# Output stage of a triangle update: the channel mean by narrow products and a subtraction, the residual added on GpSimd

## The chip, the cores and the metric

The kernel runs on one core of a Trainium2 chip. The metric is the device time of one execution in microseconds. Engines are named as in the profile: PE is TensorE, DVE is VectorE, ACT is ScalarE, POOL is GpSimd, and SP is the queue that issues most loads.

## What is computed

The input is an image of 256 x 256 positions with 128 channels in 32-bit floats. Four layers follow one another, each of the form x = x + layer(groupnorm(x)): an attention, a recurrence, a triangle update and a convolution. The change is in the triangle update's last part. Cut to what matters, the reference is:

```python
def _L2_conv_ref(pair, ...):
    pair_norm = layer_norm(pair, ln_in_w, ln_in_b)
    p = jnp.einsum('bijd,hd->bijh', pair_norm, p_in_w)
    g = jax.nn.sigmoid(jnp.einsum('bijd,hd->bijh', pair_norm, g_in_w))
    left = g[..., :H] * p[..., :H]
    right = g[..., H:] * p[..., H:]
    out = jnp.einsum('bikd,bjkd->bijd', left, right / jnp.float32(L))
    out = layer_norm(out, ln_out_w, ln_out_b)          # over the 128 channels
    out = jnp.einsum('bijh,dh->bijd', out, p_out_w)
    gate = jax.nn.sigmoid(jnp.einsum('bijd,ed->bije', pair_norm, g_out_w))
    return gate * out

# in reference():
x = x + _L2_conv_ref(_gn(x), ...)
x = x + _L3_conv_ref(_gn(x), ...)                       # the convolution, which needs x's statistics
```

The change concerns the last four lines of the layer and the residual addition: a layer norm over channels, the output product, the gate, the sum with x, and the statistics of this sum for the next group norm.

## The kernel before, in words

Channels lie on the 128 partitions, positions along the free dimension. The triangle update (method `triangle`) has three stages. The first normalises x (read from the DRAM image x2T) and writes the result to znT. The second makes left and right factors (`LR`) from znT and multiplies them; the result goes channel by channel, by stores that POOL issues, to the DRAM image prodD. The third, which the change rewrites, reads prodD, znT and x2T in 32 pieces of 2048 positions (`NB // 2`; a piece of one image is 1 MB) and writes the sum to x3T.

In the third stage all work on TensorE, VectorE and ScalarE is issued through helpers that keep the program's order (`mm`, `act`, `tt`, `stt`, `bn`, `table`), so each of these engines runs its instructions strictly as written. The loads on SP and the stores on POOL have no such tie: a scheduler places them, each in its queue's own order.

For piece p the loop does this:

- `load(p + 2)` fetches znT, prodD and x2T for two pieces ahead into tiles `zn`, `pr` and `xin`, three buffers each.
- `variance` multiplies the squares of the centred piece with `m32` (`tmean`, 128 x 32, every entry 1/128): four products of 512 columns, each into 32 partitions of one PSUM tile `var`, placed side by side in the array. Two ScalarE passes (logarithm, then exponential times -0.5) make 1/sigma, `rs`.
- `gates(p)`: product of `zn` with the gate weights (`pe`, L61 like all products), then a sigmoid on ScalarE into `ga`. It needs another table of functions than the logarithm, so each piece has two table loads.
- `spreads` brings `rs` back to all partitions: four products with 32 rows each (`tspread`), in two PSUM tiles `pr` of 1024 columns. (The name `pr` thus stands for a PSUM tile here and for the SBUF tile of the product above.)
- VectorE scales: `on` = `zs` times `pr`.
- `centre(p + 1)`: the product of the next piece with `cmat`, a full 128 x 128 matrix that subtracts the channel mean (`zc`); ScalarE copies it to `zs` and squares that into `sq`.
- `py`: the output product of `on`, then on VectorE `ga` = (`py` + bias) times `ga`, `x3` = `ga` + `xin`, and `bn` statistics of `x3`, 512 columns at a time.
- POOL issues the store of `x3` to x3T (L1361).

PSUM has two kinds of buffers here: tag `w`, three slots of 1024 columns, which `pe`, `pr`, `zc` and `py` take in turn, and tag `r`, two slots of 512 columns for `var`. A slot is taken again when its last reader is done. At piece 28, `early_statistics` combines the statistics so far on VectorE. After the last piece the convolution's group norm waits for all statistics. The tiles of this stage lie on the memory of the second stage's tiles: the first ones on the buffers of `zt` (loads of znT), the later ones on `LR`.

Of the kernel before, what the change touches and what calls it, by code (L numbers as in the profile page):

```python
# [9 lines left out]
F32 = mybir.dt.float32  # L10
AF = mybir.ActivationFunctionType
ALU = mybir.AluOpType
# [5 lines left out]
P = 128  # L18
# [8 lines left out]
LN_EXP = "natural_log_exp_and_others"  # L27
EXP_TANH = "exp_and_others"
SIGMOID = "sigmoid_and_others"


class Kernel:
# [21 lines left out]
    def act(self, out, in_, func, bias=0.0, scale=1.0, **kw):  # L54
        return self.nc.scalar.activation(out, in_, func, bias=bias, scale=scale, **kw)  # L55

    def table(self, name, key="table"):
        return self.chain(key, self.nc.scalar.preload_act_table_set(name))

    def mm(self, out, lhsT, rhs, start=True, stop=True):  # L60
        return self.nc.tensor.matmul(out, lhsT, rhs, start=start, stop=stop)  # L61
# [1067 lines left out]
    def triangle(self, x2T, x3T, znT, prodD, stats2, shift2, stats3, prepare):  # L1129
# [3 lines left out]
        nc, tc, I = self.nc, self.tc, self.i  # L1133
        V = nc.vector
        NB, G, CQ = NPIX // 1024, 4, P // 4
        pin = lambda f: lambda *a, **k: tc.keep_in_program_order(f(*a, **k))  # L1136
        mm, act, copy = pin(self.mm), pin(self.act), pin(nc.scalar.copy)
        tt, ts, stt, bn = pin(V.tensor_tensor), pin(V.tensor_scalar), pin(V.scalar_tensor_tensor), pin(V.bn_stats)
        table, add = pin(nc.scalar.preload_act_table_set), pin(V.tensor_scalar_add)
        flat = lambda t: t.rearrange("p k n -> p (k n)")  # L1140
        MUL, ADD = ALU.mult, ALU.add
        with ExitStack() as c:
            wp = c.enter_context(self.pool(name="tw", bufs=1))
            with self.pool(name="twp", bufs=2, space=PSUM) as ps0:
# [4 lines left out]
                wpg, oraw, we = W, W["o"], W["e"]  # L1149
                pb = ps0.tile([P, 2], F32, name="tpbo", tag="gn")  # L1150
                self.mm(pb[:, 0:1], oraw, lob)
                wbo = wp.tile([P, 1], F32, name="twbo")
                V.tensor_copy(wbo, pb[:, 0:1])
                wo = wp.tile([P, P], F32, name="two")
# [13 lines left out]
            m32 = wp.tile([P, 32], F32, name="tmean")  # L1168
# [4 lines left out]
            def variance(ps, work, sq):  # L1173

                var = ps.tile([P, 512], F32, name="var", tag="r", bufs=2)
                for k in range(4):
                    mm(var[32 * k:32 * k + 32], m32, sq[k // 2][:, (k % 2) * 512:(k % 2 + 1) * 512])
                rs = work.tile([P, 512], F32, name="rs")
                act(rs, var, AF.Ln, bias=self.eps)
                act(rs, rs, AF.Exp, scale=-0.5)  # L1180
                return rs

            def spreads(ps, rs):
                pr = [ps.tile([P, 1024], F32, name="pr", tag="w") for _ in range(2)]
                for k in range(4):
                    mm(pr[k // 2][:, (k % 2) * 512:(k % 2 + 1) * 512], spread[32 * k:32 * k + 32], rs[32 * k:32 * k + 32])
                return pr


            with ExitStack() as c1:  # L1190
                io = c1.enter_context(self.pool(name="t1", bufs=3))
                work = c1.enter_context(self.pool(name="t1w", bufs=4))
                ps = c1.enter_context(self.pool(name="t1s", bufs=3, space=PSUM))
                xin, sq, zs = {}, {}, {}

                def load(m):
                    if m < NB // 2:
                        xin[m] = io.tile([P, 2048], F32, name="xin")
                        nc.sync.dma_start(xin[m], x2T[:, m * 2048:(m + 1) * 2048])

                def centre(m, b):
                    if m >= NB // 2:
                        return
                    zc = ps.tile([P, 1024], F32, name="zc", tag="w")
                    for k in range(2):
                        s = b * 1024 + k * 512
                        mm(zc[:, k * 512:(k + 1) * 512], lc, xin[m][:, s:s + 512])
                    zs[m, b] = work.tile([P, 1024], F32, name="zs")
                    add(zs[m, b], zc, cb)
# [12 lines left out]
                for m in range(NB // 2):  # L1222
                    load(m + 2)
                    centre(m + 1, 0)
                    rs = variance(ps, work, [sq[m, b] for b in range(2)])
# [3 lines left out]
                    pr = spreads(ps, rs)  # L1229
# [44 lines left out]

            with ExitStack() as c1:
                io = c1.enter_context(self.pool(name="t3", bufs=3))
                work = c1.enter_context(self.pool(name="t3w", bufs=3))
                ps = c1.enter_context(self.pool(name="t3s", bufs=3, space=PSUM))
                D = [{} for _ in range(NB // 2)]

                def product(wt, src, h, name):
                    z = ps.tile([P, 2, 512], F32, name=name, tag="w")
                    for k in range(2):
                        mm(z[:, k], wt, src[:, h * 1024 + k * 512:h * 1024 + (k + 1) * 512])
                    return flat(z)

                def load(p):
                    if p < NB // 2:

                        for n, src in (("zn", znT), ("pr", prodD), ("xin", x2T)):  # L1290
                            t = D[p][n] = io.tile([P, 2048], F32, name=n)
                            for c0, c1 in ((0, 96), (96, P)) if n == "pr" and p == 0 else ((0, P),):
                                nc.sync.dma_start(t[c0:c1], src[c0:c1, p * 2048:(p + 1) * 2048])

                def centre(p):
                    if p < NB // 2:
                        d = D[p]
                        d["zs"], d["sq"] = [], []
                        for h in range(2):
                            zc = product(self.cmat, d["pr"], h, "zc")  # L1300
                            z = work.tile([P, 1024], F32, name="zs")
                            act(z, zc, AF.Copy)
                            d["zs"].append(z)
                            sq = work.tile([P, 1024], F32, name="sq")
                            act(sq, z, AF.Square)
                            d["sq"].append(sq)

                def stats(h):
                    for k in range(2):
                        o = h * 1024 + k * 512  # L1310
                        bn(stats3[:, 4 * p + 2 * h + k, :], x3[:, o:o + 512])

                def gates(p):
                    pe = [product(we, D[p]["zn"], h, "pe") for h in range(2)]
                    if p:
                        table(SIGMOID)
                    D[p]["ga"] = []
                    for h in range(2):
                        ga = work.tile([P, 1024], F32, name="ga")
                        act(ga, pe[h], AF.Sigmoid)  # L1320
                        D[p]["ga"].append(ga)

                load(0)
                load(1)
                gates(0)
                centre(0)
                table(LN_EXP)
                for p in range(NB // 2):
                    d = D[p]
                    load(p + 2)  # L1330
                    on, py, x3 = [], [], io.tile([P, 2048], F32, name="x3")
                    hs = [slice(h * 1024, (h + 1) * 1024) for h in range(2)]
                    rs = variance(ps, work, d["sq"])
                    if p:
                        gates(p)
                    pr = spreads(ps, rs)
                    for h in range(2):
                        on.append(work.tile([P, 1024], F32, name="on"))
                        tt(on[h], d["zs"][h], pr[h], MUL)
                    ga = d["ga"]  # L1340
                    centre(p + 1)
                    if p + 1 < NB // 2:
                        table(LN_EXP)
                    py = [product(wo, on[h], 0, "py") for h in range(2)]
                    last = p + 1 == NB // 2
                    if p == NB * 7 // 16:
                        self.early_statistics(stats3, "3")
                    gate = lambda h: stt(ga[h], py[h], wbo, ga[h], ADD, MUL)
                    if not last:
                        gate(0)  # L1350
                        gate(1)
                    for h in range(2):
                        if last:
                            gate(h)
                        tt(x3[:, hs[h]], ga[h], d["xin"][:, hs[h]], ADD)
                        if last:
                            stats(h)
                    for h in range(2):
                        if not last:
                            stats(h)  # L1360
                    nc.gpsimd.dma_start(x3T[:, p * 2048:(p + 1) * 2048], x3)  # L1361
                    d.clear()

    def transformed_taps(self, late, kt, wd, bv):

# [279 lines left out]
```

## Time and profile before

| What | us |
|---|---|
| median of 3 runs (4857.59 to 4860.5) | 4858.48 |
| profiled execution, whole | 4863.21 |
| its span, from the first to the last instruction | 4861.1 |
| PE busy in the span | 4680.3 (96%) |
| DVE busy | 3632.2 (75%) |
| ACT busy | 3331.2 (69%) |
| POOL busy | 1858.4 (38%) |

The profile page is one execution recorded by the hardware. A group of instructions is named by line, engine, operation and tiles (output, arrow, inputs); the line is that of the helper that issues it, so L61 stands for every product and L55 for most of ScalarE, and one goes by the tiles. The number after x is the count, and the mean duration follows in ns; then comes the idle time of the engine just before these instructions and who ended it. A product of 32-bit floats is issued as two passes, and weight loads and products are counted together in the chain, so four products of 512 columns appear as x8. The chain of waits goes back from the last instruction to whatever released it, and shows where time can be saved.

The third stage runs from 3899.5 to 4326.7 us of the span. In the timeline the first loads stand out: znT's first piece is issued at 3824.3, and the second part of prodD's first piece, which needs the last channel's store, at 3899.5.

### The profile page before, as it was taken

What the parts mean: (1) busy time and instruction counts of PE and PEld (TensorE: products, weight loads), DVE (VectorE), ACT (ScalarE), POOL (GpSimd) and SP (SyncE); (2) the same over time, 40 slices, a digit from 0 to 9 for tenths busy, and PEclk for the clock granted to TensorE, in tenths of its full rate; (3) what the DMA queues carried; (4) which work ended last, traced back from release to release, by engine and by line L of the source; (5) the groups of instructions that cost most, each with busy time, mean ns of one, the idle gap of its engine ahead of it and who ended that gap; (6) DMA issues with size and microseconds to landing.
All of it is one profiled execution on the core that took longest, in us unless ns stands there. A gap on an engine that the chain in (4) does not pass through costs nothing.

```text
span 4861.1 us, 78233 instructions
## 1 busy us (share of the span) xinstructions
PE 4680.3 (96%) x30415; PEld 2669.2 (55%) x30415; DVE 3632.2 (75%) x4551; ACT 3331.2 (69%) x5009; POOL 1858.4 (38%) x1294
## 2 busy tenths in 40 slices
PE   8999999999999899999999996999999999999999
PEld 2444555555555433333333332269999943369999
DVE  6676777777777699999999996763443367789886
ACT  6556888888888799999999995543333377752110
POOL 0344555555555376666666664421001100000000
PEclk9999999999999999999999998999999999999999
DMA  8893122222222245555555555986776598854432
GB/s 299 309 350 112 53 80 87 84 88 83 80 87 83 80 110 132 132 133 131 133 132 133 134 131 164 331 327 225 265 256 225 211 349 324 320 205 165 141 120 70
DMA packets 221153, 835.13 MB, mean 172 GB/s; under 512 B 59142, under 2 KB 62492, under 8 KB 172244
## 3 DMA queue, kind: packets, MB, share of 16 engines
q1 hardware_dynamic: 144606, 498.19, 29.9%
q0 software_dynamic: 74880, 331.50, 23.4%
q8 instruction: 244, 4.00, 0.3%
q14 instruction: 127, 1.04, 0.1%
q10 hardware_dynamic: 1296, 0.40, 0.0%
HBM read 497.84 MB, written 265.03 MB: 157 GB/s over the span
## 4 chain that ended last, share of the span: by engine, by line
PE 66%; ACT 14%; DVE 11%; issue 6%; DMA 2%; POOL 1%; SPq 0%; ACTq 0%; DVEq 0%; POOLq 0%
PE z L61 9%; PE m L61 8%; PE zc L61 7%; PE nd L61 7%; PE sc L61 6%; PE po L61 5%; PE ppq L61 3%; PE ppv L61 3%; PE pe L61 2%; PE ppg L61 2%; PE ppk L61 2%; PE px L61 2%; PE py L61 2%; PE var L61 2%; ACT L950 2%
## 5 line engine op out<-in xcount | busy, mean ns | idle before, releaser
L609 DVE TENSOR_TENSOR e<-sc,bT 128x1024 f32<-128x1024 f32 x512 | 613.2, 1218 | 255.9 <-PE sc L61 253.8
L609 POOL TENSOR_TENSOR ks<-e 128x1024 f32<-128x1024 f32 x256 | 601.4, 2367 | 443.0 <-PE nd L61 429.5
L55 ACT ACTIVATE e<-e 128x1024 f32<-128x1024 f32 x512 | 539.6, 1054 | 39.5 <-DVE e L609 29.9
L1136 DVE TENSOR_TENSOR LR<-z,sg 128x512 f32<-128x512 f32 x256 | 268.2, 1048 | 363.2 <-ACT sg L55 363.2
L61 PE MATMUL m<-U,v 128*128 128x128 f32 x4608 | 514.7, 275 | 0.0
L61 PEld LDWEIGHTS m<-U,v 128*128 128x128 f32 x4608 | 514.6, 192 | 0.0
L61 PE MATMUL z<-wf,zt 128*128 128x128 f32 x4096 | 458.4, 275 | 2.4 <-DVE zn L1136 1.4
L61 PEld LDWEIGHTS z<-wf,zt 128*128 128x128 f32 x4096 | 458.0, 192 | 3.6 <-DVE zn L1136 2.2
L55 ACT ACTIVATE sg<-z 128x512 f32<-128x512 f32 x256 | 152.8, 597 | 307.7 <-PE z L61 307.7
L1268 POOL DMA_DIRECT2D prodD<-o x128 | 69.0, 540 | 617.2 <-ACT o L55 607.4
L61 PE MATMUL sc<-proj 32*128 32x256 f32 x4096 | 300.1, 403 | 3.0 <-DVE e L609 2.2
L978 POOL TENSOR_TENSOR fs<-f 128x512 f32<-128x512 f32 x64 | 176.4, 2756 | 276.1 <-DVE f L975 256.5
L61 PEld LDWEIGHTS sc<-proj 32*128 32x128 f32 x4096 | 188.1, 185 | 160.9 <-PE px L61 94.8
L61 PE MATMUL nd<-e,proj 128*32 128x256 f32 x4096 | 272.3, 383 | 2.6 <-DVE og L609 2.6
L55 ACT ACTIVATE dn<-dn 128x512 f32<-128x512 f32 x384 | 237.8, 619 | 10.3 <-DVE dn L609 6.2
L978 POOL TENSOR_TENSOR u<-t,tr 128x512 f32<-128x512 f32 x64 | 232.4, 3632 | 11.1 <-DVE tr L981 9.7
L978 POOL TENSOR_TENSOR t<-t,v 128x1024 f32<-128x1024 f32 x64 | 209.6, 3275 | 51.9 <-DVE t L975 51.9
L61 PE MATMUL po<-LR 128*128 128x256 f32 x1024 | 222.1, 379 | 6.9 <-DVE LR L1136 6.9
L1521 ACT COPY m4s<-m 128x512 f32<-128x512 f32 x32 | 18.7, 585 | 290.5 <-PE m L61 290.5
L61 PEld LDWEIGHTS po<-LR 128*128 128x128 f32 x1024 | 194.2, 190 | 34.0 <-DVE LR L1136 7.7
L1531 POOL DMA_DIRECT2D out_dram<-ys x32 | 37.0, 1155 | 425.4 <-DVE ys L1529 425.4
L61 PE MATMUL av<-y,ident 128*128 128x512 f32 x384 | 192.2, 609 | 4.1 <-DVE y L975 4.1
(381 smaller groups left out, 10637.2 us busy)
## 6 DMA issues: line engine op xcount, KB each, us to landing
zt<-znT SPq DMA_DIRECT2D x128, 1024.0 KB
xin<-x2T SPq DMA_DIRECT2D x64, 1024.0 KB
znT<-zn POOLq DMA_DIRECT2D x61, 1024.0 KB, 5.2
xin<-in_x_dram SPq DMA_DIRECT2D x48, 1024.0 KB
xr<-x3T SPq DMA_DIRECT2D x46, 768.0 KB
x1T<-x POOLq DMA_DIRECT2D x64, 512.0 KB, 4.9
xf<-x1T SPq DMA_DIRECT2D x64, 512.0 KB
xc<-x1T SPq DMA_DIRECT2D x128, 256.0 KB
```

The source lines that it names most:

```text
L55: return self.nc.scalar.activation(out, in_, func, bias=bias, scale=scale, **kw)
L61: return self.nc.tensor.matmul(out, lhsT, rhs, start=start, stop=stop)
L609: pin = lambda f: lambda *a, **k: tc.keep_in_program_order(f(*a, **k))
L950: pin(nc.scalar.preload_act_table_set(want))
L978: pin(nc.gpsimd.tensor_tensor(out, a, b_, op))
L1136: pin = lambda f: lambda *a, **k: tc.keep_in_program_order(f(*a, **k))
L1268: nc.gpsimd.dma_start(prodD[g * CQ + d].rearrange("(p a j) -> p a j", p=P, a=2), o.rearrange("p a j b -> p a (j b)"))
L1521: nc.scalar.copy(m4, m[4])
L1531: nc.gpsimd.dma_start(out[row:row + 8].rearrange("r p t c -> p (r t) c"), ys.rearrange("p g k t c -> p (g k t) c"))
```

## The change

The centred piece is no longer the result of a full product. The channel mean is made in 32 partitions as the variance is (`mean`: four narrow products, then a ScalarE copy `mr`), spread back to all partitions by `spreads`, and subtracted from the piece in place on VectorE; ScalarE squares the result. Scaling by 1/sigma happens in place too. The residual is added by GpSimd, in place in the tile of x2T, except for the last piece, where VectorE does it. The work of a piece is now spread over four steps of the loop: its mean is made two steps ahead of its gate, centring and variance one step ahead, gate and scaling in its own step, and output product, gate multiplication, residual, statistics and store in the step after. Loads run three pieces ahead, with 6 buffers for prodD, 4 for znT and 5 for x2T; prodD comes first among them. The early statistics follow those of piece 27 in the loop.

```diff
--- before.py
+++ after.py
@@ -1274,9 +1274,18 @@
 
             with ExitStack() as c1:
                 io = c1.enter_context(self.pool(name="t3", bufs=3))
-                work = c1.enter_context(self.pool(name="t3w", bufs=3))
+                work = c1.enter_context(self.pool(name="t3w", bufs=2))
                 ps = c1.enter_context(self.pool(name="t3s", bufs=3, space=PSUM))
-                D = [{} for _ in range(NB // 2)]
+                M = NB // 2
+                zn, pd, xr, ga, sq, mr, rs = ({} for _ in range(7))
+                half = lambda t, h: t[:, h * 1024:(h + 1) * 1024]
+
+                def load(p):
+                    if p < M:
+                        for d, n, src, bufs in ((pd, "pr", prodD, 6), (zn, "zn", znT, 4), (xr, "xin", x2T, 5)):
+                            d[p] = t = io.tile([P, 2048], F32, name=n, bufs=bufs)
+                            for c0, c1 in ((0, 96), (96, P)) if n == "pr" and p < 2 else ((0, P),):
+                                nc.sync.dma_start(t[c0:c1], src[c0:c1, p * 2048:(p + 1) * 2048])
 
                 def product(wt, src, h, name):
                     z = ps.tile([P, 2, 512], F32, name=name, tag="w")
@@ -1284,82 +1293,78 @@
                         mm(z[:, k], wt, src[:, h * 1024 + k * 512:h * 1024 + (k + 1) * 512])
                     return flat(z)
 
-                def load(p):
-                    if p < NB // 2:
-
-                        for n, src in (("zn", znT), ("pr", prodD), ("xin", x2T)):
-                            t = D[p][n] = io.tile([P, 2048], F32, name=n)
-                            for c0, c1 in ((0, 96), (96, P)) if n == "pr" and p == 0 else ((0, P),):
-                                nc.sync.dma_start(t[c0:c1], src[c0:c1, p * 2048:(p + 1) * 2048])
+                def gates(p):
+                    if p < M:
+                        pe = [product(we, zn[p], h, "pe") for h in range(2)]
+                        table(SIGMOID)
+                        ga[p] = [work.tile([P, 1024], F32, name="ga", bufs=5) for _ in range(2)]
+                        for h in range(2):
+                            act(ga[p][h], pe[h], AF.Sigmoid)
+
+                def mean(p):
+                    if p < M:
+                        mn = ps.tile([P, 512], F32, name="mn", tag="r", bufs=2)
+                        for k in range(4):
+                            mm(mn[32 * k:32 * k + 32], m32, pd[p][:, k * 512:(k + 1) * 512])
+                        mr[p] = work.tile([P, 512], F32, name="mr")
+                        act(mr[p], mn, AF.Copy)
 
                 def centre(p):
-                    if p < NB // 2:
-                        d = D[p]
-                        d["zs"], d["sq"] = [], []
+                    if p < M:
+                        mb = spreads(ps, mr[p])
+                        sq[p] = [work.tile([P, 1024], F32, name="sq") for _ in range(2)]
                         for h in range(2):
-                            zc = product(self.cmat, d["pr"], h, "zc")
-                            z = work.tile([P, 1024], F32, name="zs")
-                            act(z, zc, AF.Copy)
-                            d["zs"].append(z)
-                            sq = work.tile([P, 1024], F32, name="sq")
-                            act(sq, z, AF.Square)
-                            d["sq"].append(sq)
-
-                def stats(h):
+                            tt(half(pd[p], h), half(pd[p], h), mb[h], ALU.subtract)
+                            act(sq[p][h], half(pd[p], h), AF.Square)
+
+                def output(p):
+                    py = [product(wo, pd[p], h, "py") for h in range(2)]
+                    for h in range(2):
+                        stt(ga[p][h], py[h], wbo, ga[p][h], ADD, MUL)
+                        (tt if p == M - 1 else pin(nc.gpsimd.tensor_tensor))(half(xr[p], h), ga[p][h], half(xr[p], h), ADD)
+                        if p == M - 1:
+                            stats(p, h)
+
+                def scale(p):
+                    if p < M:
+                        pr = spreads(ps, rs[p])
+                        for h in range(2):
+                            tt(half(pd[p], h), half(pd[p], h), pr[h], MUL)
+
+                def root(p):
+                    if p < M:
+                        table(LN_EXP)
+                        rs[p] = variance(ps, work, sq[p])
+
+                def stats(p, h):
                     for k in range(2):
                         o = h * 1024 + k * 512
-                        bn(stats3[:, 4 * p + 2 * h + k, :], x3[:, o:o + 512])
-
-                def gates(p):
-                    pe = [product(we, D[p]["zn"], h, "pe") for h in range(2)]
-                    if p:
-                        table(SIGMOID)
-                    D[p]["ga"] = []
-                    for h in range(2):
-                        ga = work.tile([P, 1024], F32, name="ga")
-                        act(ga, pe[h], AF.Sigmoid)
-                        D[p]["ga"].append(ga)
-
-                load(0)
-                load(1)
+                        bn(stats3[:, 4 * p + 2 * h + k, :], xr[p][:, o:o + 512])
+
+                for p in range(3):
+                    load(p)
                 gates(0)
+                mean(0)
                 centre(0)
-                table(LN_EXP)
-                for p in range(NB // 2):
-                    d = D[p]
-                    load(p + 2)
-                    on, py, x3 = [], [], io.tile([P, 2048], F32, name="x3")
-                    hs = [slice(h * 1024, (h + 1) * 1024) for h in range(2)]
-                    rs = variance(ps, work, d["sq"])
+                root(0)
+                mean(1)
+                for p in range(M + 1):
+                    load(p + 3)
                     if p:
                         gates(p)
-                    pr = spreads(ps, rs)
-                    for h in range(2):
-                        on.append(work.tile([P, 1024], F32, name="on"))
-                        tt(on[h], d["zs"][h], pr[h], MUL)
-                    ga = d["ga"]
                     centre(p + 1)
-                    if p + 1 < NB // 2:
-                        table(LN_EXP)
-                    py = [product(wo, on[h], 0, "py") for h in range(2)]
-                    last = p + 1 == NB // 2
-                    if p == NB * 7 // 16:
-                        self.early_statistics(stats3, "3")
-                    gate = lambda h: stt(ga[h], py[h], wbo, ga[h], ADD, MUL)
-                    if not last:
-                        gate(0)
-                        gate(1)
-                    for h in range(2):
-                        if last:
-                            gate(h)
-                        tt(x3[:, hs[h]], ga[h], d["xin"][:, hs[h]], ADD)
-                        if last:
-                            stats(h)
-                    for h in range(2):
-                        if not last:
-                            stats(h)
-                    nc.gpsimd.dma_start(x3T[:, p * 2048:(p + 1) * 2048], x3)
-                    d.clear()
+                    if p:
+                        output(p - 1)
+                    scale(p)
+                    root(p + 1)
+                    mean(p + 2)
+                    if p:
+                        if p < M:
+                            stats(p - 1, 0)
+                            stats(p - 1, 1)
+                        nc.gpsimd.dma_start(x3T[:, (p - 1) * 2048:p * 2048], xr[p - 1])
+                        if p == M * 7 // 8:
+                            self.early_statistics(stats3, "3")
 
     def transformed_taps(self, late, kt, wd, bv):
 
```

## The prediction

> **What bounds the kernel now.** I read the page's parts 1 and 2 first: TensorE is busy for 96% of the span, so a change pays only where TensorE's own queue gets shorter. The stage that changes runs from 3899.5 us (first gate product) to 4326.7 us (end of the last statistics: 4325.44 + 1.29). Then I read the chain of waits in this stage, since it names what each moment waits for; columns are start, length, engine and tile.
>
> ```profile
> 4002.53 1.30 PE pr L61 x8
> 4003.83 3.63 PE zc L61 x8
> 4007.46 3.43 PE py L61 x8
> 4010.89 0.99 PE var L61 x8
> 4011.89 3.63 PE pe L61 x8
> 4015.52 1.30 PE pr L61 x8
> ```
>
> The chain holds TensorE alone, without a gap: from pr at 4002.53 to pr at 4015.52 is 12.99 us for one piece of 2048 columns, and it repeats for all pieces. The groups by form in this window show how far the other engines are from that.
>
> ```profile
> L1136 DVE SCALAR_TENSOR_TENSOR ga<-py,twbo,ga 128x1024 f32<-128x1024 f32 x64 | 82.1, 1283 | 106.9 <-PE py L61 106.9
> L1136 ACT ACT_TABLE_LOAD x63 | 80.8, 1283 | 1.1
> L1136 DVE BATCH_NORM_STATS2 stats<-x 128x6 f32<-128x512 f32 x126 | 77.7, 678 | 0.0
> L1136 DVE TENSOR_TENSOR on<-zs,pr 128x1024 f32<-128x1024 f32 x64 | 74.7, 1207 | 9.6 <-PE pr L61 9.5
> L1136 DVE TENSOR_TENSOR x<-ga,xin 128x1024 f32<-128x1024 f32 x63 | 74.1, 1217 | 0.0
> L55 ACT ACTIVATE zs<-zc 128x1024 f32<-128x1024 f32 x64 | 64.9, 1014 | 69.6 <-PE zc L61 69.6
> ```
>
> VectorE waits on TensorE for 107 us here, ScalarE for 70 us: both have room. Last, the stretches: busy time by engine, then granted clock, DMA share and GB/s.
>
> ```profile
> 3899.00:3950.00 51.00, 47.50 (x144) 18.23 (x144) 30.98 (x40) 36.76 (x38) 1.19 (x3) 1.00 0.97 384
> 3950.00:4000.00 50.00, 50.00 (x157) 19.62 (x156) 35.90 (x39) 37.63 (x39) 2.00 (x4) 1.00 0.96 362
> 4000.00:4100.00 100.00, 100.00 (x307) 39.39 (x306) 72.56 (x78) 76.02 (x78) 4.25 (x8) 1.00 0.87 320
> ```
>
> TensorE is full, VectorE 73%, ScalarE 76%, GpSimd almost empty at 4%; the DMA engines stand at 0.87 and are the second limit to watch.
>
> **What the Trainium skill says.** "SBUF — State Buffer", Who interferes with whom: a VectorE instruction with two SBUF inputs contends with a GpSimd instruction that reads SBUF, one with at most one SBUF input (outside the 2-port modes) doesn't. The trace agrees: `ks<-e` on GpSimd takes 2349 to 2391 ns while VectorE adds scores from PSUM, but `u<-t,tr`, half as long, takes 3632 ns beside two-input SBUF work of the recurrence. "TensorEngine Tiling (Array Packing)", Key Properties: changing the tiling mode drains TensorE. The trace agrees in size: full products right after narrow ones cost 3.63 (pe, zc), py after zc only 3.43. "SBUF — State Buffer", Summary, advises some 358 GB/s for HBM to SBUF; here 384 GB/s were moved over 51 us, so the measurement decides.
>
> **The change, part by part, for one piece.**
>
> *TensorE.* Removed: zc, 3.63. Added: mn, four 128-to-32 products in the very form of var; var costs 1.00 with its switch, and mn follows var in the same mode, so I take 0.90 (estimate; 8 passes at the 0.43 pitch of the full products, four tiles side by side, give 0.86; upper end 1.00). Added: a second pr, 1.30. py now follows a row-tiled product and pays the switch: 3.63 for 3.43. var follows pr instead of py: I keep 1.00 (it could be 0.9 to 1.3; scores followed by narrow sums in the attention stage pay no more than pr does here). Sum: pe 3.63 + pr 1.30 + py 3.63 + pr 1.30 + var 1.00 + mn 0.90 = 11.76, against 12.99: 1.23 less; ends 11.6 and 12.1.
>
> *Does anything else end later than TensorE?* I lay one period out, pe at 0, with the durations above and the gaps of the timeline (first half of a full product to its reader 2.0, pr to its reader 1.40).
> - ScalarE: the logarithm of var starts at -0.76, two passes of 0.69 and 0.63, mr until 1.2 (0.59, as `m4s<-m`, 585 ns), table load until 2.5, ga until 3.55 and 4.77. The second pr (mean) needs the first ga by 3.6, py the second by 4.93: they hold, as zc's wait for ga held before.
> - VectorE: subtract 5.03 to 7.4 (2 x 1.2), gates 7.4 to 10.0 (2 x 1.28), multiply 10.0 to 12.4, statistics 12.4 to 14.9 (2.46 for four). The next subtract can begin at 11.76 + 5.03 = 16.8: 1.9 us spare.
> - ScalarE again: squares 6.25 to 8.5, table load to 9.8; var starts at 9.86.
> - PSUM tag w has three slots for eight tiles a piece. Closest is the second half of pr (1/sigma), whose slot is free when the first gate has read py at 8.7; it would start near 8.7 to 8.9. I cost it at nothing; if all latencies stack, 0.3.
> VectorE's total is unchanged: a subtract (1.2) comes for each residual add (1.22) that leaves. ScalarE loses two copies (2.03) and gains mr (0.59): worth nothing, as TensorE covers both.
>
> *GpSimd.* Two adds by 2.37 from the `ks<-e` row (4.74), plus the store's 0.53: 5.3 of 11.76. In this window no VectorE row of the new steady loop has two SBUF inputs: the subtraction and the scaling read PSUM beside SBUF, so does the gate, and the statistics read one tile. First add 8.8 to 11.15, second to 13.6; the third statistics instruction wants it at 13.65, with 1.9 us behind it before anyone on TensorE notices. The x3T store is queued behind the adds and leaves at 13.6, some 2.6 us later relative to its gate than before; its landing (10.5 us) frees an xin buffer for the load five pieces on, which has over a period to spare. Bounds for one add: 2.37 to 3.3 costs nothing (1.9 / 2 above), more is paid for.
>
> *SP and the DMA queues.* Bytes don't change: 4 MB a piece, 323 GB/s at 12.99 and 357 at 11.76. SP's order is now pr, zn, xin with pr two pieces ahead and xin behind the store of five pieces before. From 3899.5, at 390 GB/s (2.7 us per MB), pr of piece 2 lands near 3916, wanted at 3920; pr of piece 3 at 3924, wanted at 3932; piece 4 at 3932, wanted at 3943. So a lead is built before the stores start, and I cost the loads at nothing.
>
> *Start.* zn of piece 0 was fetched at 3824; now its buffer lies over LR, so it waits for the last po product (chain: 3840.32 + 55.52 = 3895.84). With 5.2 us for a 1 MB store as the nearest row, the first pe starts near 3901 instead of 3899.46: 1.5 lost. Then the chain pe, mn, ga, mr, pr, subtract, square, var, logarithm, mr, pr, subtract, square, var, mn brings pe of piece 1 to 3921.2 to 3921.4; before it stood at 3920.87, as py of piece 0 is not yet due. Loss: 0.4.
>
> *End.* Thirty periods from 3921.3 give 352.8, less one mn (0.9), plus the early aggregate, which now meets VectorE's spare 1.9 us with 3.18 + 0.17 of work: 1.4. So iteration 31 starts at 4274.6. From there by the same rows: pe, py of piece 30, pr; multiply ends 10.9, statistics of piece 30 at 13.4, then gate, add and statistics of both halves of piece 31, 2 x (1.28 + 1.22 + 1.29), to 21.0: 4295.6. Before: 4326.7. Gain 31.1 us. The convolution's first loads and products hang on these statistics as before, and its length stays.
>
> Against the profiled execution (span 4861.1, whole 4863.2) that is 4830.0 and 4832.1. The median of the runs, 4858.5, lies 4.7 below that execution, so the forecast is 4858.5 - 31.1 = 4827.
>
> **The rivals.**
> - *DMA becomes the bound.* For: a share of 0.87 at 320 GB/s scales to 0.97 at 357. Against: 362 and 384 GB/s were reached here with the same traffic. If it holds at 340 GB/s, a piece takes 12.3 and the gain falls by 30 x 0.54 to 15: 4843.
> - *Slots and mode switches.* One more switch a piece and the wait of pr for the gate, 0.4 together: 12.16, gain 19: 4839. For: the margins of 0.1 to 0.2 above. Against: zc's equal margin cost nothing.
> - *GpSimd's add is slow* (the slower side). VectorE runs in order, so its statistics hold up the next subtraction: subtract to end of first gate 3.7, two adds 2a, two statistics and latencies 1.4, thus a loop of 5.1 + 2a. At 2.37 that is 9.8, hidden. It decides from a = 3.3 and is slower than before from a = 3.95. At the rate of `u<-t,tr` (3.63 for 512, so 7.26) a piece takes 19.6, and 31 pieces add 205: 5063. Against: the instructions beside it have one SBUF input each.
> - *The mean isn't narrow*, its four products running one after the other. var, the same form, shows 1.00 for four: I give it nothing.
>
> **How the numbers follow.** Forecast 0.74, DMA 0.09, slots and switches 0.10, slow add 0.07. A change within 0.2% (9.7 us) can't be told from none; 0.02 of the two middle cases falls there. Faster 0.91, same 0.02, slower 0.07. The forecast alone spans 4819 to 4835 (period 11.6 to 12.0); to hold 8 in 10 the range takes in the middle of the two rivals: 4818 to 4843.
>
> **What would show it.** Chain: TensorE alone at 11.7 to 11.9 a piece, pe 3.63, pr 1.30 twice, py 3.63, var and mn near 1. The GpSimd add at 2.3 to 2.5 us, VectorE idle before the subtraction, released by pr. A DMA share of 0.95 without DMA in the chain. First pe near 3901. It is wrong if xin (GpSimd) or a load stands in the chain, or if the add takes over 3.3 us.

## The result and the profile after

The changed kernel takes 4823.82 us (median of 4 runs, 4821.62 to 4824.02) against 4858.65 for the kernel before in the same call: 34.8 us less, a ratio of 0.9927 with a 95% interval of 0.991 to 0.9944. Run again in another call, beside the experiments, it took 4822.31 against 4861.17: 38.9 us less, 0.9923 (0.991 to 0.9937). The forecast was 4827, a gain of 31.1.

The chain of waits after, one piece and the start of the next (start, length, engine and tile). Each x8 counts the two passes of four products; the weight loads aren't in it, they are counted apart as PEld.

```profile
4002.78 3.65 PE pe L61 x8
4006.42 0.02 issue
4006.44 0.02 ACTq L55
4006.46 0.04 issue
4006.50 1.03 ACT ga L55
4007.54 0.04 issue
4007.58 3.70 PE py L61 x8
4011.28 1.07 PE pr L61 x8
4012.35 1.00 PE var L61 x8
4013.35 0.86 PE mn L61 x8
4014.21 3.65 PE pe L61 x8
```

From pe to pe it is 14.21 - 2.78 = 11.43 us a piece, for 12.99 before. Nearly all of it is TensorE. One other engine now appears: py follows the second gate's sigmoid on ScalarE, and the pr that spreads the mean has vanished from the chain, because it fits into the time that this sigmoid takes. From the end of pe to py it is 4007.58 - 4006.42 = 1.16 us.

The groups by form from 4000 to 4200 us show what VectorE and GpSimd wait for:

```profile
L1136 POOL TENSOR_TENSOR xin<-ga,xin 128x1024 f32<-128x1024 f32 x36 | 84.5, 2363 | 105.6 <-DVE ga L1136 105.6
L1136 DVE TENSOR_TENSOR pr<-pr 128x1024 f32<-128x1024 f32 x70 | 82.1, 1215 | 27.7 <-PE pr L61 27.7
L1136 DVE BATCH_NORM_STATS2 stats<-xin 128x6 f32<-128x512 f32 x72 | 44.4, 679 | 0.0
```

The GpSimd add takes 2363 ns, as the forecast took it (2367), and the statistics never wait for it (0.0). The group `pr<-pr` holds the subtractions and the scalings; in the timeline VectorE waits before the subtractions, 1.63 us a piece, for TensorE's `pr`. The stretches (busy time by engine in the order PE, weight load, DVE, ACT, POOL, then granted clock, DMA share and GB/s):

```profile
3950.00:4000.00 50.00, 49.48 (x208) 17.32 (x208) 41.48 (x44) 37.08 (x40) 21.36 (x13) 1.00 0.99 400
4000.00:4100.00 100.00, 99.07 (x427) 34.08 (x424) 82.70 (x88) 74.20 (x79) 47.13 (x27) 1.00 0.98 377
```

VectorE went from 73% to 83%, GpSimd from 4% to 47%, the DMA share from 0.87 to 0.98. That last figure looks like a limit, and two experiments below ask whether it is one.

To compare runs I measure the stage in each profile from the first product after the second stage (`cpb`) to the last aggregate of the statistics: 3895.67 to 4326.77 before, so 431.1 us; 3894.44 to 4287.07 after, so 392.6. The stage is 38.5 us shorter in the profiles. Times below stand beside the kernel before in the same call.

| Kernel | stage, us | us a piece | median, us | before, us | difference |
|---|---|---|---|---|---|
| changed | 392.6 | 11.43 | 4823.82 | 4858.65 | -34.8 |
| changed, again | 393.5 | 11.43 | 4822.31 | 4861.17 | -38.9 |
| before, again | 431.4 | 12.99 | 4857.98 | 4862.42 | one run |
| before, only the residual moved | 431.2 | 13.00 | 4861.79 | 4860.67 | +1.1 |
| changed, full product for the mean | 424.3 | 12.56 | 4855.02 | 4862.42 | -7.4 |
| changed, residual on VectorE | 410.4 | 11.80 | 4840.86 | 4862.42 | -21.6 |
| changed, half the gate input | 389.1 | 11.43 | 4818.67 | 4862.42 | -43.8 |
| changed, 0.25 MB more a piece | 410.9 | 11.43 to 15.8 | 4843.08 | 4860.67 | -17.6 |
| changed, the same load spaced | 395.5 | 11.43 | 4824.07 | 4861.17 | -37.1 |
| changed, five prodD buffers | 394.0 | 11.43 | 4822.76 | 4861.17 | -38.4 |
| changed, GpSimd adds doubled | 505.3 | 14.9 (mean) | 4935.19 | 4860.67 | +74.5 |
| changed, gate input first | 392.9 | 11.43 | 4821.45 | 4860.67 | -39.2 |
| changed, first loads in order of need | 392.5 | 11.43 | 4816.93 | 4861.17 | -44.2 |

### The profile page after: what moved, and what is told of

Read it like the earlier page. It is cut to its first block, busy times and chain, and to the rows that moved or that the text cites. A ratio compares the mean times of both kernels' runs of the same rounds, so it can differ in the third digit from the quotient of the medians.

```text
span 4821.7 us, 78838 instructions
## 1 busy us (share of the span) xinstructions
PE 4634.6 (96%) x30671; PEld 2636.5 (55%) x30671; DVE 3635.7 (75%) x4553; ACT 3288.8 (68%) x4978; POOL 2007.2 (42%) x1356
## 4 chain that ended last, share of the span: by engine, by line
PE 66%; ACT 15%; DVE 11%; issue 6%; DMA 2%; POOL 1%; SPq 0%; ACTq 0%; DVEq 0%; POOLq 0%
PE z L61 10%; PE m L61 8%; PE nd L61 7%; PE sc L61 6%; PE zc L61 5%; PE po L61 5%; PE ppq L61 3%; PE ppv L61 3%; PE pe L61 2%; PE py L61 2%; PE ppg L61 2%; PE ppk L61 2%; PE px L61 2%; PE var L61 2%; ACT L950 2%
## 5 line engine op out<-in xcount | busy, mean ns | idle before, releaser
L609 POOL TENSOR_TENSOR ks<-e 128x1024 f32<-128x1024 f32 x256 | 601.6, 2367 | 442.5 <-PE nd L61 429.0
L1136 POOL TENSOR_TENSOR xin<-ga,xin 128x1024 f32<-128x1024 f32 x62 | 145.5, 2363 | 210.2 <-DVE ga L1136 210.2
```

## The experiments

The theory: the narrow products shorten TensorE's queue, which sets the period, and everything else only has to stay out of the way. The rivals: the gain comes from relieving VectorE or from the new pipeline; or the DMA engines set the period.

**The kernel before once more.** No edit.

> The kernel before, unchanged, for a second profile beside the first. Every theory expects 12.99 us a piece again; the question is where the 4.7 us lie by which the first profiled execution exceeded the median. If the stage is the same length again (430.9 us from the last po product to the last statistics), they lie outside of it.

4857.98 us with a span of 4855.9. The stage is 431.4 us, as long as in the first profile. The stage starts 4.0 us earlier (3891.66 for 3895.67), so most of the excess of the first profiled execution lay ahead of this stage and has nothing to do with it.

**Only the residual moved.** In the kernel before:

```diff
-                        tt(x3[:, hs[h]], ga[h], d["xin"][:, hs[h]], ADD)
+                        (tt if last else pin(nc.gpsimd.tensor_tensor))(x3[:, hs[h]], ga[h], d["xin"][:, hs[h]], ADD)
```

> The kernel before with only its residual add moved to GpSimd (last piece on VectorE). Theory of narrow products: TensorE's queue is untouched, 12.99 us a piece and 4858, within 2 us. Theory that relieving VectorE brings the gain: 10 us or more faster.

```profile
4000.00:4100.00 100.00, 100.00 (x312) 39.05 (x311) 58.39 (x63) 77.01 (x78) 41.97 (x24) 1.00 0.85 323
```

Ratio 1.0 (0.9991 to 1.0008). VectorE's load falls from 73 to 58 us in 100 and the period stays. In the old loop the relief of VectorE alone is worth nothing.

**Full product for the mean, all else as changed.** The narrow mean goes (with it the two calls of `mean` ahead of the loop); the full product with `cmat` and ScalarE's copy return:

```diff
-                        mb = spreads(ps, mr[p])
...
-                            tt(half(pd[p], h), half(pd[p], h), mb[h], ALU.subtract)
+                            act(half(pd[p], h), product(self.cmat, pd[p], h, "zc"), AF.Copy)
...
-                    mean(p + 2)
```

> The changed kernel with centring by the full product again (copied back in place by ScalarE), pipeline and residual on GpSimd kept. Theory of narrow products: TensorE pe 3.63 + zc 3.43 + py 3.43 + pr 1.07 + var 1.00 = 12.56 us a piece if a bare pr costs 1.07 (12.79 if it costs 1.30 everywhere), so 34 us (or 41) above the changed kernel: near 4858 (4865). Theory that pipeline and GpSimd residual bring the gain: 4824 to 4835.

The chain of waits of this run:

```profile
4071.83 3.63 PE pe L61 x8
4075.46 3.43 PE zc L61 x8
4078.90 3.43 PE py L61 x8
4082.33 1.07 PE pr L61 x8
4083.40 1.00 PE var L61 x8
4084.40 3.63 PE pe L61 x8
```

12.56 us a piece, as summed with pr at 1.07. So the pipeline with the residual on GpSimd brings 12.99 - 12.56 = 0.43: zc now follows a full product instead of a narrow one (3.43 for 3.63), and pr stands without the wait behind it (1.07 for 1.30). In time that is little: ratio 0.9986 (0.9979 to 0.9993), 7.4 us. Thirty periods bring 12.7 us; in the profile 1.3 of them are lost again by pe of piece 1 and 4.6 after pe of piece 31, as each piece now ends one step later. The narrow mean then brings 12.56 - 11.43 = 1.13 a piece and most of the gain (424.3 to 392.6 us of stage). The pipeline as the cause of the gain falls as a rival.

**Residual back on VectorE, all else as changed.**

```diff
-                        (tt if p == M - 1 else pin(nc.gpsimd.tensor_tensor))(half(xr[p], h), ga[p][h], half(xr[p], h), ADD)
+                        tt(half(xr[p], h), ga[p][h], half(xr[p], h), ADD)
```

> The changed kernel with only the residual back on VectorE (in place). VectorE then holds 2.35 + 2.34 + 2.56 + 2.40 + 2.46 = 12.1 us of work a piece in one queue, more than TensorE's 11.43. Theory of narrow products with VectorE as the next limit: 12.1 to 12.4 us a piece, 20 to 30 us slower than the changed kernel, near 4844 to 4854. If the move to GpSimd gave nothing: 4824.

```profile
4000.00:4100.00 100.00, 99.61 (x402) 34.23 (x401) 99.44 (x104) 71.77 (x76) 4.64 (x9) 1.00 0.95 361
```

```profile
L1136 DVE TENSOR_TENSOR pr<-pr 128x1024 f32<-128x1024 f32 x68 | 79.5, 1209 | 0.0
```

In this run's stretch VectorE (third pair of numbers) is full, 99.44 of 100, and the period 11.80. TensorE looks as full (99.61), but its groups are stretched: pe takes 3.84 for 3.65, the second pr 1.29 for 1.07. VectorE no longer waits for TensorE before `pr<-pr` (groups by form from 4000 to 4200 us: 0.0, for 27.7 in the changed kernel). So VectorE is the next limit. The period is less than the 12.1 that I had summed, because in the timeline many of VectorE's instructions start 0.08 us before the one ahead ends: from start to start the same instructions fill 11.80. Ratio 0.9955 (0.9939 to 0.9972), so 13 to 17 us of the gain are lost. The residual's move is worth nothing in the old kernel and this much in the new one.

**Half the gate input.** Only the first half of each znT piece is loaded, and both gate products read it; the kernel leaves out the second half's own gates:

```diff
+                            w = 1024 if n == "zn" else 2048
...
+                                nc.sync.dma_start(t[c0:c1, :w], src[c0:c1, p * 2048:p * 2048 + w])
...
-                        pe = [product(we, zn[p], h, "pe") for h in range(2)]
+                        pe = [product(we, zn[p], 0, "pe") for h in range(2)]
```

> The changed kernel with half of each znT piece left unloaded; both gate products read the first half, so the second half's gates are not those of the reference. The DMA engines carry 3.5 MB a piece instead of 4, all else stays. Theory of TensorE as the bound: 11.43 us a piece and 4822 to 4825 (at most 1 to 2 us less at the start). Theory that DMA at a share of 0.98 sets the period: 10.0 to 10.5 possible for DMA, so the piece falls to TensorE's own 11.35 or less and loads leave the chain; 4 us or more faster.

```profile
4000.00:4100.00 100.00, 99.07 (x421) 34.24 (x423) 82.36 (x88) 74.52 (x78) 44.57 (x27) 1.00 0.88 322
4100.00:4200.00 100.00, 99.07 (x422) 34.42 (x411) 82.70 (x89) 74.56 (x80) 45.73 (x27) 1.00 0.86 318
```

The DMA share (last but one) falls to 0.88 and the period stays at 11.43, with the same sigmoid in the chain. So the DMA engines didn't set the period. The run is faster all the same, 0.991 (0.9894 to 0.9927), by 3.5 us of stage: all of it is at the start, where pe of piece 1 stands 24.8 us after `cpb` in place of 28.3. My figure of 1 to 2 us for the start was too small; the run pointed to what the last ones try.

**A quarter MB more a piece.** A load that nobody reads, in the changed kernel:

```diff
+                        x = io.tile([P, 512], F32, name="extra", bufs=1)
+                        nc.sync.dma_start(x, x2T[:, p * 2048:p * 2048 + 512])
```

> The changed kernel with 0.25 MB more to load for each piece (512 columns of x2T into a tile that nobody reads). 4.25 MB a piece is 390 GB/s at 11.43 us. Theory of TensorE as the bound with DMA room up to the 400 GB/s seen while the buffers filled: 11.43 us a piece, within 3 us of the changed kernel. Theory that DMA is at its limit at 370 to 377 GB/s: a piece takes 11.8 to 12.1 us, 12 to 20 us slower, and loads appear in the chain.

Ratio 0.9966 (0.9952 to 0.9979): slower than the changed kernel, at first sight as the DMA theory has it. The timeline of SP tells otherwise:

```profile
4018.10 0.80 SPq L1288 DMA_DIRECT2D xin<-x2T  x1
4018.99 0.83 SPq L1288 DMA_DIRECT2D zn<-znT  x1
4020.71 0.32 SPq L1291 DMA_DIRECT2D extra<-x2T  x1
4021.08 0.43 SPq L1288 DMA_DIRECT2D pr<-prodD  x1
4027.54 6.18 SPq L1291 DMA_DIRECT2D extra<-x2T  x2
4033.82 0.37 SPq L1288 DMA_DIRECT2D xin<-x2T  x1
```

The loads aren't tied to an order, and the extra ones, which have no reader, came early: three for every piece's loads in this stretch, and all 32 were issued by 4107 us. Each waits for the one before to land in the single buffer, with the needed loads queued behind. SP's own waits from 4036 to 4121 us (sum, times, longest) show it:

```profile
SPq L1291 <- DMA extra<-x2T: 58.1, 15, 8.5
```

The six pieces in this stretch took 12.8 to 15.8 us, the others 11.43, while the DMA engines moved less than in the changed kernel (348 GB/s for 377). The run measured a blocked queue and not bandwidth, so the next one has another form.

**The same load, spaced, and its measure.** 0.5 MB for every second piece; each tile is given back when GpSimd has read one column of it in that piece's output step. Five buffers for prodD make the room, so a run with only that stands beside it:

```diff
-(pd, "pr", prodD, 6)
+(pd, "pr", prodD, 5)
...
+                        if p % 2 == 0:
+                            extra[p] = io.tile([P, 1024], F32, name="extra", bufs=2)
+                            nc.sync.dma_start(extra[p], x2T[:, p * 2048:p * 2048 + 1024])
...
+                    if p in extra:
+                        pin(nc.gpsimd.tensor_copy)(work.tile([P, 1], F32, name="seen"), extra[p][:, 0:1])
```

> As the quarter-MB run, but spaced: for every second piece 0.5 MB more to load, each tile given back only when GpSimd has read one column of it in that piece's output step; five buffers for prodD in place of six make the room. 4.25 MB a piece on average, 390 GB/s at 11.43 us. If DMA has room up to 400 GB/s: 11.43 us a piece and at most 3 us over the run with five buffers alone. If the limit is 370 to 377: 11.8 to 12.1 us a piece, 12 us or more slower than it.

> The changed kernel with five buffers for prodD in place of six, as a measure for the run before it. Loads run several pieces ahead, so 11.43 us a piece and within 2 us of the changed kernel. If it is slower by more, the lead of the loads is what the deep buffers were for.

```profile
4000.00:4100.00 100.00, 99.18 (x421) 34.53 (x422) 84.09 (x89) 74.36 (x79) 47.71 (x31) 1.00 1.00 408
4100.00:4200.00 100.00, 99.07 (x424) 34.18 (x426) 82.37 (x87) 74.08 (x78) 45.69 (x30) 1.00 1.01 392
```

4824.07 us beside 4822.76 with five buffers alone, and 11.43 us a piece in both. At a share of 1.00 the engines still moved 392 to 408 GB/s in these stretches, and the kernel didn't wait for data. The run with the blocked queue went higher still once its extra loads were through, at a period of 11.43:

```profile
4121.00:4200.00 79.00, 78.28 (x332) 27.16 (x328) 62.88 (x68) 58.52 (x61) 33.76 (x20) 1.00 1.01 424
```

How much more it would take is open.

**GpSimd's add doubled.** Two adds of 512 columns into an unread tile ahead of each residual add:

```diff
+                            for k in range(2):
+                                junk = work.tile([P, 512], F32, name="junk", bufs=1)
+                                pin(nc.gpsimd.tensor_tensor)(junk, ga[p][h][:, k * 512:(k + 1) * 512], half(xr[p], h)[:, k * 512:(k + 1) * 512], ADD)
```

> The changed kernel with two more GpSimd adds of 512 columns ahead of each residual add, into a tile that nobody reads: an add then stands for 2.36 + 2 x 1.25 = 4.9 us. Theory of the VectorE loop (5.1 + 2a): 14.9 us a piece, 3.4 more, about 104 us slower, near 4928, with VectorE's statistics waiting for GpSimd. If statistics waiting on GpSimd cost nothing because TensorE runs ahead: GpSimd's own 2 x 4.9 + 0.57 = 10.4 fits below 11.43 and the time stays 4824.

```profile
L1136 POOL TENSOR_TENSOR junk<-ga,xin 128x512 f32<-128x512 f32 x52 | 66.0, 1268 | 53.9 <-DVE ga L1136 51.9
L1136 DVE BATCH_NORM_STATS2 stats<-xin 128x6 f32<-128x512 f32 x54 | 34.7, 685 | 67.5 <-POOL xin L1136 67.5
```

The groups by form from 4000 to 4200 us show an add of 2.36 + 2 x 1.27 = 4.9, the statistics waiting for GpSimd (67.5 us, zero before), and a mean period of 14.9: the loop of 5.1 + 2a to a tenth. The chain of waits of this run goes round this loop: the two adds on GpSimd, then VectorE's statistics, subtraction and gate, then GpSimd again. GpSimd's own work, some 10.4 us a piece, would have fitted below 11.43; it is the order of VectorE's queue that makes it costly. Ratio 1.0156 (1.014 to 1.0171); the median, 4935.19, is 7 us above the 4928 expected.

**The start.** In the changed kernel znT's first tile lies over LR and comes late. Two edits: znT first in the load, so that it takes an early free buffer; then the first nine loads in the order in which they are needed (`fetch` loads one piece of one image; prodD of piece 2 now comes in two parts as well).

```diff
-((pd, "pr", prodD, 6), (zn, "zn", znT, 4), (xr, "xin", x2T, 5))
+((zn, "zn", znT, 4), (pd, "pr", prodD, 6), (xr, "xin", x2T, 5))
```

```diff
-                for p in range(3):
-                    load(p)
+                for n, p in (("zn", 0), ("pr", 0), ("pr", 1), ("pr", 2), ("zn", 1), ("xin", 0), ("zn", 2), ("xin", 1), ("xin", 2)):
+                    fetch(n, p)
```

> The changed kernel with znT first in the load, so that its first tile lies on a buffer that is free early and not on LR. Theory that the start lost its time to this one load: the first pe begins within 4 us of the last po product as in the kernel before (it was 6.0 after it, and took 5.3 at a lower clock), the stage is 3 to 5 us shorter, near 4820. If the start is set by prodD's last channels instead: no change, 4824.

> The changed kernel with the first loads in the order of need: znT of piece 0 on an early free buffer, then prodD of pieces 0, 1 and 2, then znT and x2T. Theory that the start is lost to loads (znT over LR in the changed kernel; prodD of piece 1 behind two other loads once znT came first): the first pe within 4 us of the last po product, no wait of TensorE for prodD, the clock kept, and pe of piece 1 some 25 us after the last po product, not 28.3; 3 to 5 us faster than the changed kernel. If the chain of operations alone sets the start: no change.

> The changed kernel itself, on the chip of the three runs beside it. Every theory: 11.43 us a piece, some 35 us below the kernel before.

With znT first the first pe starts 3.8 us after `cpb`, not 6.2, but pe of piece 1 comes no earlier, 28.6 us for 28.3. The chain and the stretch from 3910 to 3918 us show two reasons:

```profile
3897.26 11.32 DMA pr<-prodD
3908.58 0.14 issue
3908.72 1.97 PE mn L61 x8
```

```profile
3910.00:3918.00 8.00, 7.29 (x28) 2.42 (x28) 4.52 (x4) 3.77 (x4) 0.00 (x0) 0.50 1.01 416
```

TensorE now waits for prodD of piece 1, third in line, if only for 0.91 us (timeline); and its granted clock (last but two) is 0.50 from 3904 to 3920 us. From the first `var` to pe of piece 1 it took 15.8 us, 11.5 in the changed kernel. In the order of need the wait for prodD is gone: 4816.93 us (five runs, four of them 4816.69 to 4817.31) beside 4822.31 (4819.88 to 4825.92) for the changed kernel on the same chip. The ratios to the kernel before are 0.9911 (0.9897 to 0.9924) and 0.9923 (0.991 to 0.9937); their intervals overlap, so the 5.4 us are likely rather than proven. The profiled execution of this run was the slowest of the five (4824.09): its pe of piece 1 came 27.5 us after `cpb`, with TensorE at a granted clock of 0.50 from 3910 to 3918 us, and from the first `var` to this pe it still took 14.7 us. The data were in time, the clock wasn't. Its stage, 392.5 us, is no shorter than the changed kernel's, and none of the four faster executions has a profile, so where they save the 5.4 us isn't shown.

## Why the prediction was right

- *TensorE's sum.* The mechanism was right, one term was mis-sized. I took pr at 1.30 twice, from the chain of before. There its length hides a wait: the weight loads of zc, which came next, idled for the sigmoid on ScalarE (groups by form of the kernel before, in the stage):

```profile
L61 PEld LDWEIGHTS zc<-pr,cmat 128*128 128x128 f32 x256 | 46.0, 189 | 70.0 <-issue 38.7 <-ACT ga L55 23.5 <-DVE on L1136 7.6
```

  A bare pr costs 1.07, shown twice over (after, and with the full product). The first pr with its sigmoid costs 1.16, the second 1.07, against 2.60 in my sum: 0.37 a piece. pe came to 3.65 and py to 3.70 for 3.63, mn to 0.86 for 0.90, var to 1.00. Together 11.43 for 11.76, below the 11.6 to 12.1 that I gave; over 30 periods 10 us more gain. So of the signs that I named, a period of 11.7 to 11.9 and TensorE alone in the chain didn't come; the add, the idle time before the subtraction and the DMA share did.
- *What hides behind TensorE.* Right: ScalarE's and VectorE's edits cost nothing, and the add at 2363 ns kept clear of the statistics. The 1.9 us of spare time for VectorE was well sized: the early aggregate cost 13.03 - 11.43 = 1.6 us for the 1.4 predicted.
- *The start.* Too small: 0.4 us was taken, and pe of piece 1 moved from 25.2 to 28.3 us after `cpb`, 3.1 lost (3.9 in the second profile). The forecast had pe of piece 1 25.6 us after `cpb`. Of the 2.7 us that it missed, 0.8 is that the first pe started 6.2 us after `cpb` and not 5.3, and 1.6 that the granted clock was 0.50 for the first 3 us of this pe, which was not foreseen:

```profile
3900.61 5.31 PE L61 MATMUL pe<-zn,w2e 128*128 128x512 f32 x8 [3.61 <-DMA zn<-znT]
```

  That is 5.31 us for 3.70, after 3.61 us of waiting for znT (timeline of the changed kernel).
- *The end.* From pe of piece 31 to the last aggregate 20.7 us, for 21.0.
- *The rivals.* DMA: its share rose to 0.98 as worked out (0.97), and it set nothing. Slots and switches: no wait in TensorE's steady part beyond the sigmoid's 0.1. The slow add: it didn't happen, but its loop and its price were right, as doubling the add showed.

The errors partly cancel, and to that extent the nearness of the forecast is luck: 10 us of gain too little for the period, some 3 of loss too little for the start. The stage in the profiles is 38.5 us shorter, the medians of two calls 34.8 and 38.9 apart; the forecast had 31.1.

## What to carry to other kernels

A group's length in the chain of waits ends where the next group starts: before carrying it into a sum, look whether the next group idled for another engine, and take a bare instance if there is one. Moving work to an idle engine was worth nothing here until the bound moved, and 13 to 17 us then; what it costs is set by who waits for it in order, not by the idle engine's own total. A transfer share near one is no verdict; halve or add bytes, in the order in which the kernel needs them.

## What the runs showed of the hardware

- After a wait at the start of the stage TensorE can run at half of its clock. In all eleven profiles of the rewritten loop the granted clock falls to 0.50, for 3 to 17 us at a time, and each fall begins within 1.6 us of the end of a wait of TensorE that lasted 2.45 to 3.61 us. In the three profiles of the old loop (before, again, only the residual moved), whose waits there last at most 1.61 us, it stays at 1.00. The stretch from 3910 to 3918 us of the kernel before, of the changed kernel and of the run with its first loads in order:

```profile
3910.00:3918.00 8.00, 6.39 (x22) 2.69 (x21) 2.35 (x2) 4.75 (x7) 0.00 (x0) 1.00 1.02 419
```

```profile
3910.00:3918.00 8.00, 5.70 (x28) 1.63 (x28) 1.79 (x3) 5.20 (x6) 0.00 (x0) 0.79 1.00 387
```

```profile
3910.00:3918.00 8.00, 7.30 (x28) 1.99 (x24) 1.09 (x1) 3.60 (x5) 0.00 (x0) 0.50 1.00 380
```

  The clock is 1.00, 0.79 and 0.50. A wait of this length doesn't always lower it: in the run with the spaced load TensorE waited 3.22 us for znT, and the pe behind it took 3.67 us, at full clock. Nor do the runs show why the same wait of 2.46 us was followed by 3 us at half clock in the changed kernel and by 17 in the run with its first loads in order. What decides is not settled here.
- With loads and stores of 1 MB side by side the DMA engines moved 400 GB/s over 50 us in the changed kernel, 408 GB/s over 100 us with the spaced extra load, and 424 GB/s over 79 us in the run with the blocked queue, once its extra loads were through.
